# Layer 3 of a fused four-layer kernel: values in tiles of 128 tokens, taken through DRAM

## The chip, the cores and the metric

One core of a Trainium2 chip. The metric is the device time of one execution in microseconds, as the median of several runs; beside it stands one execution taken with the hardware profiler. All data are float32.

## The reference

Four residual layers over x of shape (4, 56, 56, 256): x = x + layer(group norm of x). Layers 0 and 2 are neighbourhood attentions, layer 1 is an all-to-all similarity over tokens, layer 3 is a shifted window attention. Layer 3, the one that the change is about, cut to what matters:

```python
xs = jnp.roll(x, (-3, -3), axis=(1, 2))                    # x: normalised, (4, 56, 56, 256)
xw = windows_of_7x7(xs)                                    # (4 * 64, 49, 256)
qkv = xw @ qkv_weight.T + qkv_bias
q, k, v = split_in_8_heads_of_32(qkv);  q = q * 32 ** -0.5
attn = softmax(q @ k.T + bias + mask)                      # 49 x 49 in each window and head
out = (attn @ v) @ proj_weight.T + proj_bias
x = x + roll_back(out)
```

## The kernel before, in words

The four layers run one after the other on one core; x goes through DRAM between them, with the 256 channels as two halves (`CC` = 2) of 128 partitions and the tokens along the free axis. A Python helper, `run` at the end of the program, opens each layer's pools and traces it. The framework sets semaphores, lays out memory and orders instructions by a cost model; layers 1 and 3 take the order of the engines named in their `run` call from the text instead. For layer 3 these are TensorE (PE), VectorE (DVE), ScalarE (ACT) and GpSimd (POOL). The queue that issues the DMAs, SP, is ordered by the cost model in all layers.

Layer 3 handles an image (3136 tokens) in 8 rows of 8 windows, `WC` = 392 tokens a row, 32 rows in all. In a row the windows lie in pairs of 98 tokens.

- `load(r)` brings the tokens of a row from DRAM, `prepare(r)` normalises them into `xn` in the order of the windows (line 939, DVE), six operations for the two halves.
- `project_rows(r)` gives six steps: keys, queries and values, each twice. Keys and queries are 128 x 392 outputs (`project`, line 945), taken out of PSUM by ACT (lines 1983, 1987). Values, `value_rows` (lines 956 to 965), are computed with the tokens as output partitions: for each pair of windows one accumulation of 98 tokens by 256 channels (line 962), two pairs per step, taken out by one DVE addition of the bias (line 964) into a tile `v` of 98 partitions by 4 pairs by 256. Each matmul of float32 is two records in the trace.
- `quad(r, hq)` is one unit of attention: four heads of a row, four window pairs. `attend_quads` runs the units, two per row and 64 in all: the logits of unit w (line 1025), the closing step `done` of the unit before the last (reciprocal, line 2006, and multiplication, line 2008, on DVE), then the unit's list of filling steps, then the products of unit w - 1 with the values and with ones (line 1040). Exponentials are on ACT (1029, 1031), the mask is added on DVE (1030) for two heads and multiplied on POOL (1032) for the other two.
- `stream` writes the filling steps of each unit: a step of the output projection of row r - 2 (`project_out`, PE line 945, ACT 2028, POOL 2030), three of the six steps of row r + 1, and in the second unit of a row `prepare(r + 2)`.

So in each unit PE runs: logits, output projection, keys, queries, values, products. PSUM banks for all projections come from one pool `m` of two banks; the products have one double bank `o`. Tiles of the pool `early` outlive the seam between layers (`x`, `xn`, `w_qkv` of layer 3), which lets them be filled while layer 2 still runs; which addresses a layer's pools get depends on their sizes, since the pools of odd layers are packed from the other end of the memory than those of even layers, and a tile waits for the old tiles that it lies on.

Layers 0 and 2 compute values in another helper, `value_tiles` (lines 973 to 993): tiles of 128 tokens counted from the start of the image, without regard to the rows. Where a row ends inside a tile, the rest (`left`) is copied by ACT in front of the next row's `xn`. A step a = 0 or 1 does up to two tiles. After step 1 the row's tiles go to a DRAM tile `vd` in one DMA (line 991), and a second (993) for the half tile at the end of an image; the attention gathers its keys' values from there (lines 1237 and 1790).

The lines that a sentence can't say, from `stream`:

```python
rows = lazily(project_rows, r + 1, 6) if r + 1 < n else []
out = project_out(r - 2) if r > 1 else []
for hq in range(CC):
    steps = out[hq:hq + 1] + rows[3 * hq:3 * hq + 3]
    if hq and r + 2 < n:
        steps.append(lambda r=r: prepare(r + 2))
    steps.append(step_stats)
```

Of the kernel before, what the change touches and what calls it, by code (L numbers as in the profile page):

```python
# [830 lines left out]
def direct_blocks(ctx: ExitStack, tc: tile.TileContext, d: dict, watch):  # L831
# [121 lines left out]
        else:  # L953
            nc.scalar.copy(dst, src)

    def value_rows(v, a, n, xn, w, bias):

        pm = ps_m()
        for j in range(2):
            k = 2 * a + j  # L960
            for h in range(CC):
                nc.tensor.matmul(pm[:n, j * C:(j + 1) * C], lhsT=xn[:, h, k * n:(k + 1) * n],  # L962
                                 rhs=w[:, h, :], start=(h == 0), stop=(h == CC - 1))
        nc.vector.tensor_tensor(v[:, 2 * a:2 * a + 2, :], pm[:n, :].rearrange("p (j c) -> p j c", c=C),
                                bias[:n].rearrange("p (o c) -> p o c", o=1).to_broadcast([n, 2, C]), ALU.add)

    def left(c, n):

        return c * n % P

    def value_tiles(v, a, c, n, xn, w, bias, dst):

        t0, t1 = c * n // P, (c + 1) * n // P if (c + 1) * n < T else -(-T // P)
        pm = ps_m()
        sizes = [min(P, T - t * P) for t in range(t0, t1)]
        mine = sizes[2 * a:2 * a + 2]
        for j, k in enumerate(mine):
            first = (2 * a + j) * P  # L980
            for h in range(CC):
                nc.tensor.matmul(pm[:k, j * C:(j + 1) * C], lhsT=xn[:, h, first:first + k], rhs=w[:, h, :],  # L982
                                 start=(h == 0), stop=(h == CC - 1))
        for k in sorted(set(mine)):
            js = [j for j, kj in enumerate(mine) if kj == k]
            nc.vector.tensor_tensor(
                v[:k, 2 * a + js[0]:2 * a + js[-1] + 1, :], pm[:k, js[0] * C:(js[-1] + 1) * C].rearrange("p (j c) -> p j c", c=C),
                bias[:k].rearrange("p (o c) -> p o c", o=1).to_broadcast([k, len(js), C]), ALU.add)
        if a == 1:
            whole = sizes.count(P)  # L990
            nc.sync.dma_start(out=dst[t0 * P:(t0 + whole) * P, :].rearrange("(k p) c -> p k c", p=P), in_=v[:, :whole, :])
            if whole < len(sizes):
                nc.sync.dma_start(out=dst[(t0 + whole) * P:T, :], in_=v[:sizes[-1], whole, :])

    def seen(rs):

# [937 lines left out]
    def layer3(early, big, pool, brief):  # L1934
        def image_rows(wr):

            return [(0, 7, 7 * wr + 3)] if wr < 7 else [(0, 4, S - 4), (4, 3, 0)]

        def transfer(l, r, x, out):
            b, wr = divmod(r, 8)  # L1940
            for i0, n, r0 in image_rows(wr):
                ends = x[:, :, i0 * S:(i0 + n) * S], tokens_of(l, b, r0 * S, n * S)
                nc.sync.dma_start(out=ends[out], in_=ends[1 - out])

        xs, xns, qkv, attns = {}, {}, {}, {}

        def load(r):
            xs[r] = early.tile([P, CC, WC], FP, tag="x", name="x3")
            transfer(3, r, xs[r], 0)

        load(0)
        w_qkv = weight(early, "wqkv3", 3 * C)
        m3 = big.tile([98, 2, NH, 4 * 98], FP, name="m3l")
        nc.sync.dma_start(out=m3, in_=m3d.rearrange("p a h w k -> p a h (w k)"))
        w_p = weight(pool, "wp3", C)

        def parts(win, x):

            win = win.rearrange("p (w i j) -> p w i j", i=7, j=7)
            img = x.rearrange("p (r c) -> p r c", c=S)  # L1960
            yield (win[:, 0:7].rearrange("p w i j -> p i w j"), img[:, :, 3:52].rearrange("p r (w j) -> p r w j", j=7))
            yield win[:, 7, :, 0:4], img[:, :, 52:56]
            yield win[:, 7, :, 4:7], img[:, :, 0:3]

        def prepare(r):
            x = xs.pop(r)
            if r + 1 < NIMG * 8:
                load(r + 1)
            xn = xns[r] = early.tile([P, CC, WC], FP, tag="xn", name="xn3")
            for h in range(CC):  # L1970
                for w, xv in parts(xn[:, h, :], x[:, h, :]):
                    normalise(w, xv, known(3, r // 8), h)

        def project_rows(r):
            xn = xns.pop(r)
            qT = pool.tile([P, CC, WC], FP, tag="q", name="q3")
            kT = pool.tile([P, CC, WC], FP, tag="k", name="k3")
            v = pool.tile([98, 4, C], FP, tag="v", name="v3")
            qkv[r] = qT, kT, v

            def keys(m):
                pm = project(w_qkv, C + m * P, lambda h: xn[:, h, :], WC)
                nc.scalar.activation(kT[:, m, :], pm, AF.Identity, bias=bk3[:, m:m + 1])

            def queries(m):
                pm = project(w_qkv, m * P, lambda h: xn[:, h, :], WC)
                nc.scalar.activation(qT[:, m, :], pm, AF.Identity, bias=qbias[:, 2, m:m + 1], scale=SCALE)

            def values(a):
                value_rows(v, a, 98, xn, w_qkv[:, :, 2 * C:], bv3)  # L1990

            return [lambda f=f, m=m: f(m) for m in range(2) for f in (keys, queries, values)]

        def quad(r, hq):
            b, wr = divmod(r, 8)
            qT, kT, v = qkv[r]
            box = {}

            def output(k, u):
                if k + u == 0:  # L2000
                    box["o"] = psum_tile("o", 1, 2)
                return box["o"][:, k, u * 98:(u + 1) * 98]

            def finish():
                rs = pool.tile([P, WC], FP, tag="rs", name="rs3")
                nc.vector.reciprocal(rs, box["o"][:, 1, :WC])
                seen(rs)
                nc.vector.scalar_tensor_tensor(attns[r][:, hq, :], box["o"][:, 0, :WC], 1.0, rs, ALU.mult, ALU.mult,
                                               accum_out=watch[2][:, 2 * r + hq:2 * r + hq + 1])

            def piece(u):
                sl = slice(u * 98, (u + 1) * 98)
                return (lambda j: kT[hr(j), hq, sl], lambda j: qT[hr(j), hq, sl],
                        lambda j: v[:, u, (4 * hq + j) * HD:(4 * hq + j + 1) * HD], True, True)

            mk = m3[:, wr // 7, 4 * hq:4 * hq + 4, :]
            i = 2 * (NIMG * 8 + r) + hq
            return dict(pieces=[piece(u) for u in range(4)], nk=98, nq=98, width=WC, mask=mk[:, 0:2, :],
                        emask=mk[:, 2:4, :], sum=watch[2][:98, i:i + 1], o=output, first=no_step, done=finish)

        def project_out(r):
            x = pool.tile([P, CC, WC], FP, tag="xr", name="xr3")
            transfer(3, r, x, 0)

            def step(m):
                pm = project(w_p, m * P, lambda h: attns[r][:, h, :], WC)
                pr = pool.tile([P, WC], FP, tag="pr", name="pr3")
                nc.scalar.activation(pr, pm, AF.Identity, bias=bp3[:, m:m + 1])  # L2028
                for w, xv in parts(pr, x[:, m, :]):
                    nc.gpsimd.tensor_tensor(xv, xv, w, ALU.add)  # L2030
                if m:
                    transfer(4, r, x, 1)
            return [lambda m=m: step(m) for m in range(CC)]

        def stream():
            n = NIMG * 8
            for r in range(n):
                attns[r] = pool.tile([P, CC, WC], FP, tag="attn", name="attn3", bufs=3)
                rows = lazily(project_rows, r + 1, 6) if r + 1 < n else []
                out = project_out(r - 2) if r > 1 else []  # L2040
                for hq in range(CC):
                    steps = out[hq:hq + 1] + rows[3 * hq:3 * hq + 3]
                    if hq and r + 2 < n:
                        steps.append(lambda r=r: prepare(r + 2))
                    steps.append(step_stats)
                    w = quad(r, hq)
                    w["fill"] = lambda steps=steps: [f() for f in steps]
                    yield w

        prepare(0)  # L2050
        prepare(1)
        for step in project_rows(0):
            step()
        attend_quads(pool, stream())
        for r in range(NIMG * 8 - 2, NIMG * 8):
            for step in project_out(r):
                step()
# [125 lines left out]
```

## Time and profile before

| | us |
|---|---|
| three runs | 4051.37, 4060.95, 4060.51 |
| their median | 4060.51 |
| the profiled execution, its own time | 4046.79 |
| its span in the trace | 4044.6 |
| layer 2: first matmul of its values | 2806.5 |
| layer 3: first matmul of its keys | 3492.4 |
| layer 3: last start of an output projection | 4035.8 |
| PE busy, of the span | 3858.0 (95%) |
| DVE, ACT, POOL busy | 2364.8, 1375.9, 1741.2 |
| granted PE clock, mean | 0.978 |

All times in the trace count from the span's start. PE, PEld are TensorE's matmuls and its loads of weights, which overlap; a matmul's length is modelled and overlaps its neighbours, so that the distance of starts says more than the mean. "Idle before" is time that an engine stood still ahead of an operation, with what ended it. Names of tiles stand as out<-in, with numbers left out; shapes are partitions x elements. A stage row has PE, PEld, DVE, ACT and POOL busy in a stretch (with the number of instructions), then the granted PE clock, the DMA engines' busy share and GB/s.

### The profile page before, as it was taken

How to read it: one execution, taken by the hardware profiler on the slowest of the kernel's cores; microseconds unless marked ns; L12 is line 12 of the kernel's file. 1: busy time of each engine (PE TensorE's matmuls, PEld its weight loads, DVE VectorE, ACT ScalarE, POOL GpSimd, SP SyncE). 2: the span in 40 equal slices, each digit the busy share in tenths (PEclk: the TensorE clock that was granted, in tenths of full speed). 3: DMA queues.
4: the chain of work that ended last, by engine and by line, in shares of the span. 5: the costliest groups of instructions: out<-in, count | busy, mean ns of one | idle time of the engine just before them, and what ended most of it. 6: DMA issues, size and time to landing. Idle time of an engine off the chain costs nothing.

```text
span 4044.6 us, 92225 instructions
## 1 busy us (share of the span) xinstructions
PE 3858.0 (95%) x38983; PEld 2715.6 (67%) x38983; DVE 2364.8 (58%) x4427; ACT 1375.9 (34%) x2899; POOL 1741.2 (43%) x1883
## 2 busy tenths in 40 slices
PE   6999999899999999999999999999999999999998
PEld 4566666557777577775777757776676676666665
DVE  6777777634444444444344543445788877666665
ACT  3355555322222122222222212222555555344443
POOL 2566767621123211232112321123676777545544
PEclk9899999899999999999999999999999999999999
DMA  8443333320000000000000000001444443322221
GB/s 266 102 133 121 114 118 105 104 85 6 24 23 29 25 6 24 15 29 25 6 24 15 29 19 10 10 10 50 126 128 131 125 119 113 102 73 73 74 77 62
DMA packets 241072, 276.12 MB, mean 68 GB/s; under 512 B 23430, under 2 KB 233000, under 8 KB 240168
## 3 DMA queue, kind: packets, MB, share of 16 engines
q1 hardware_dynamic: 240362, 270.06, 21.5%
q8 instruction: 308, 5.05, 0.5%
q14 instruction: 114, 0.93, 0.1%
q10 hardware_dynamic: 288, 0.08, 0.0%
HBM read 190.55 MB, written 79.53 MB: 67 GB/s over the span
## 4 chain that ended last, share of the span: by engine, by line
PE 48%; DVE 4%; POOL 2%; issue 1%; SPq 0%; DMA 0%; ACT 0%; DVEq 0%; POOLq 0%; ACTq 0%
PE ps_m L945 12%; PE ps_o L1505 6%; PE ps_s L1421 6%; PE ps_v L1510 6%; PE ps_o L1100 3%; PE ps_m L962 3%; PE ps_s L1071 3%; PE ps_o L1040 2%; PE ps_m L982 2%; PE ps_t L1491 1%; PE ps_s L1025 1%; DVE rs L1796 1%; PE ps_m L1389 1%; DVE xn L939 0%; DVE e L1078 0%
## 5 line engine op out<-in xcount | busy, mean ns | idle before, releaser
L1433 DVE TENSOR_TENSOR acc<-acc,ps_v 128x257 f32<-128x257 f32 x1104 | 455.8, 421 | 686.5 <-PE ps_v L1510 671.7
L1510 PE MATMUL ps_v<-xw,e 128*128 128x257 f32 x2208 | 613.1, 382 | 19.7 <-DVE acc L1433 18.0
L1505 PE MATMUL ps_o<-xw,at 128*128 128x257 f32 x2208 | 609.0, 379 | 0.0
L1421 PE MATMUL ps_s<-xnT,xd 128*128 128x512 f32 (+3 forms) x1344 | 571.1, 547 | 0.0
L1494 ACT COPY at<-ps_t 128x512 f32<-128x512 f32 (+3 forms) x332 | 170.5, 514 | 1049.8 <-PE ps_t L1491 1049.8
L1510 PEld LDWEIGHTS ps_v<-xw,e 128*128 128x128 f32 x2208 | 408.6, 189 | 171.1 <-issue 80.4
L1091 POOL TENSOR_TENSOR b<-e 126x336 f32<-126x336 f32 (+5 forms) x512 | 500.0, 997 | 10.0 <-ACT e L1079 1.9
L1505 PEld LDWEIGHTS ps_o<-xw,at 128*128 128x128 f32 x2208 | 419.1, 190 | 60.1
L1414 POOL TENSOR_SCALAR xd<-xnT,vec 128x128 f32<-128x128 f32 x192 | 115.1, 610 | 632.2 <-PE ps_s L1421 629.7
L945 PE MATMUL ps_m<-xn,w_wqkv 128*128 128x392 f32 x1024 | 381.6, 507 | 3.9 <-DVE xr L1831 2.5
L1082 POOL TENSOR_TENSOR e<-e,m0t 126x672 f32<-126x672 f32 (+3 forms) x128 | 238.7, 1865 | 265.0 <-ACT e L1081 252.1
L1082 POOL TENSOR_TENSOR e<-e,bias 119x784 f32<-119x784 f32 (+5 forms) x128 | 244.4, 1909 | 180.9 <-ACT e L1081 179.7
L1421 PEld LDWEIGHTS ps_s<-xnT,xd 128*128 128x128 f32 x1344 | 225.5, 191 | 134.8 <-issue 126.2
L1424 ACT ACTIVATE e<-ps_s 128x512 f32<-128x512 f32 x336 | 185.3, 551 | 336.7 <-PE ps_s L1421 336.7
L1003 ACT ACTIVATE no<-rs 128x168 f32<-128x168 f32 (+2 forms) x256 | 93.9, 367 | 590.2 <-DVE rs L1796 273.2
L945 PEld LDWEIGHTS ps_m<-xn,w_wqkv 128*128 128x128 f32 x1024 | 190.0, 192 | 127.5 <-ACT pr L2028 17.2
L1100 PEld LDWEIGHTS ps_o<-e,vp 124*32 124x32 f32 (+3 forms) x8192 | 176.3, 110 | 141.6 <-issue 93.0
L1100 PE MATMUL ps_o<-e,vp 124*32 124x112 f32 (+3 forms) x8192 | 238.8, 253 | 6.2 <-POOL e L1082 4.4
L939 DVE TENSOR_SCALAR xn<-x,gst 128x28 f32<-128x28 f32 (+5 forms) x368 | 208.1, 619 | 35.2 <-PE ps_m L945 28.7
L1079 ACT ACTIVATE e<-e 126x672 f32<-126x672 f32 (+5 forms) x256 | 219.5, 857 | 19.0 <-DVE e L1078 6.0
L1796 DVE RECIPROCAL rs<-ps_o 128x196 f32<-128x196 f32 (+2 forms) x128 | 176.0, 1375 | 77.7 <-PE ps_o L1100 77.1
L1032 POOL TENSOR_TENSOR e<-e,m3l 98x784 f32<-98x784 f32 x64 | 118.2, 1846 | 235.7 <-ACT e L1029 212.5
(197 smaller groups left out, 6340.9 us busy)
## 6 DMA issues: line engine op xcount, KB each, us to landing
x<-xr SPq DMA_DIRECT2D x64, 392.0 KB
x<-in_x SPq DMA_DIRECT2D x53, 448.0 KB
x<-x SPq DMA_DIRECT2D x60, 392.0 KB
xr<-x SPq DMA_DIRECT2D x60, 392.0 KB
vd<-v SPq DMA_DIRECT2D x48, 384.0 KB
xr<-in_x SPq DMA_DIRECT2D x32, 392.0 KB
xr<-x SPq DMA_DIRECT2D x28, 448.0 KB
x<-xr SPq DMA_DIRECT2D x28, 448.0 KB
```

The source lines that it names most:

```text
L939: nc.vector.tensor_scalar(dst, src, gst[:, h, 0:1], gst[:, h, 1:2], ALU.subtract, ALU.mult)
L945: nc.tensor.matmul(pm[:, :n], lhsT=w[:, h, col:col + P], rhs=rhs(h), start=(h == 0), stop=(h == CC - 1))
L1079: nc.scalar.activation(ev, ev, AF.Exp)
L1082: nc.gpsimd.tensor_tensor(parts(ev), parts(ev), w["emask"], ALU.mult)
L1091: nc.gpsimd.tensor_tensor(w["b"][a][:nk, :, :2 * nq].rearrange("p h (i c) -> p h i c", i=2), ev[:, :, :, 0, :], ev[:, :, :, 1, :], ALU.add)
L1100: nc.tensor.matmul(w["o"](k, i)[j * HD:(j + 1) * HD], lhsT=ones[:nk, :HD] if k else v(j, u), rhs=w["b"][j // 2][:nk, j % 2, i * nq:(i + 1) ...
L1421: nc.tensor.matmul(s[:, :n], lhsT=xd[j][:, h, :], rhs=xnT[:, h, first * P:last * P], start=(h == 0), stop=(h == CC - 1))
L1424: nc.scalar.activation(e[:, :n], s[:, :n], AF.Exp, scale=5.0)
L1433: nc.vector.tensor_tensor(acc[:, i, :], acc[:, i, :], pv[:, :C + 1], ALU.add)
L1505: nc.tensor.matmul(out[j][:, :C + 1], lhsT=e[:, col(i)] if i == j else at[:, col(i)], rhs=xw[:, i, :], start=(i == j), stop=(i == NB - 1))
L1510: nc.tensor.matmul(pv[:, :C + 1], lhsT=e[:, col(i)], rhs=xw[:, j, :], start=True, stop=True)
L1796: nc.vector.reciprocal(rs.rearrange("p (t c) -> p t c", t=2), pv[:, :, 1, :])
```

## The change

`value_rows` goes; layer 3 computes its values with `value_tiles`, as layers 0 and 2 do, and takes them through DRAM.

- `xn` becomes 448 wide with three buffers; `prepare` normalises behind the rest of the row before and copies that rest in front (ACT). It runs one row earlier, three ahead of the attention.
- `values(r)` makes the row's three tiles (four at the end of an image) in two steps, two rows ahead of the attention, into a tile `vt` of one buffer, and writes them to `vd`. With step 0 of a row the row before is complete, and `gather` reads its 392 tokens back as 98 partitions by 4 pairs, the form that the products take, into `vs`.
- `project_rows` keeps keys and queries (four steps). In a unit the steps stand as: output projection, keys, queries, values, `prepare`.
- Ahead of the first unit stand the values of rows 0 and 1, then keys and queries of row 0, then `prepare(2)`.
- `value_tiles` itself writes to DRAM after each addition and no longer once per row. Layers 0 and 2 use it too: in the built program their stores to `vd` are 128 where they were 68.

```diff
 def value_tiles(v, a, c, n, xn, w, bias, dst):
...
             bias[:k].rearrange("p (o c) -> p o c", o=1).to_broadcast([k, len(js), C]), ALU.add)
-        if a == 1:
-            whole = sizes.count(P)
-            nc.sync.dma_start(out=dst[t0 * P:(t0 + whole) * P, :].rearrange("(k p) c -> p k c", p=P), in_=v[:, :whole, :])
-            if whole < len(sizes):
-                nc.sync.dma_start(out=dst[(t0 + whole) * P:T, :], in_=v[:sizes[-1], whole, :])
+            t = t0 + 2 * a + js[0]
+            nc.sync.dma_start(out=dst[t * P:min((t + len(js)) * P, T), :].rearrange("(k p) c -> p k c", p=k),
+                              in_=v[:k, 2 * a + js[0]:2 * a + js[-1] + 1, :])
...
-        xs, xns, qkv, attns = {}, {}, {}, {}
+        xs, xns, vs, qk, attns, ahead = {}, {}, {}, {}, {}, []
+        vd = [dram.tile([T, C], FP, name=f"vd3_{b}") for b in range(NIMG)]
...
-            xn = xns[r] = early.tile([P, CC, WC], FP, tag="xn", name="xn3")
+            c = r % 8
+            xn = xns[r] = early.tile([P, CC, 448], FP, tag="xn", name="xn3", bufs=3)
+            at = left(c, WC)
             for h in range(CC):
-                for w, xv in parts(xn[:, h, :], x[:, h, :]):
+                for w, xv in parts(xn[:, h, at:at + WC], x[:, h, :]):
                     normalise(w, xv, known(3, r // 8), h)
+            if at:
+                end = left(c - 1, WC) + WC
+                nc.scalar.copy(xn[:, :, :at], ahead[0][:, :, end - at:end])
+            ahead[:] = [xn]
...
-            def values(a):
-                value_rows(v, a, 98, xn, w_qkv[:, :, 2 * C:], bv3)
-
-            return [lambda f=f, m=m: f(m) for m in range(2) for f in (keys, queries, values)]
+            return [lambda f=f, m=m: f(m) for m in range(2) for f in (keys, queries)]
+
+        def gather(r):
+
+            b, c = divmod(r, 8)
+            vs[r] = pool.tile([98, 4, C], FP, tag="v", name="v3")
+            nc.sync.dma_start(out=vs[r], in_=vd[b][c * WC:(c + 1) * WC, :].rearrange("(k p) c -> p k c", p=98))
+
+        def values(r):
+
+            b, c = divmod(r, 8)
+            xn = xns[r]
+            v = pool.tile([P, 4, C], FP, tag="vt", name="vt3", bufs=1)
+
+            def step(a):
+                value_tiles(v, a, c, WC, xn, w_qkv[:, :, 2 * C:], bv3, vd[b])
+                if a == 0 and r:
+                    gather(r - 1)
+                if a and r == NIMG * 8 - 1:
+                    gather(r)
+            return [lambda a=a: step(a) for a in range(2)]
...
-                rows = lazily(project_rows, r + 1, 6) if r + 1 < n else []
+                rows = lazily(project_rows, r + 1, 4) if r + 1 < n else []
+                ahead_values = lazily(values, r + 2, 2) if r + 2 < n else []
                 out = project_out(r - 2) if r > 1 else []
                 for hq in range(CC):
-                    steps = out[hq:hq + 1] + rows[3 * hq:3 * hq + 3]
-                    if hq and r + 2 < n:
-                        steps.append(lambda r=r: prepare(r + 2))
+                    steps = out[hq:hq + 1] + rows[2 * hq:2 * hq + 2] + ahead_values[hq:hq + 1]
+                    if hq and r + 3 < n:
+                        steps.append(lambda r=r: prepare(r + 3))
                     steps.append(step_stats)
...
         prepare(0)
         prepare(1)
+        for r in range(2):
+            for step in values(r):
+                step()
         for step in project_rows(0):
             step()
+        prepare(2)
         attend_quads(pool, stream())
```

More of the change, by code (lines that the diff above doesn't have):

```diff
@@ L954, in evac @@
             nc.scalar.copy(dst, src)
[L956 to L965, printed above, removed]
     def left(c, n):
@@ L1968, in prepare @@
                 load(r + 1)
-            xn = xns[r] = early.tile([P, CC, WC], FP, tag="xn", name="xn3")
+            c = r % 8
+            xn = xns[r] = early.tile([P, CC, 448], FP, tag="xn", name="xn3", bufs=3)
+            at = left(c, WC)
             for h in range(CC):
-                for w, xv in parts(xn[:, h, :], x[:, h, :]):
+                for w, xv in parts(xn[:, h, at:at + WC], x[:, h, :]):
                     normalise(w, xv, known(3, r // 8), h)
+            if at:
+                end = left(c - 1, WC) + WC
+                nc.scalar.copy(xn[:, :, :at], ahead[0][:, :, end - at:end])
+            ahead[:] = [xn]
         def project_rows(r):
-            xn = xns.pop(r)
+            at = left(r % 8, WC)
+            xn = xns.pop(r)[:, :, at:at + WC]
             qT = pool.tile([P, CC, WC], FP, tag="q", name="q3")
             kT = pool.tile([P, CC, WC], FP, tag="k", name="k3")
-            v = pool.tile([98, 4, C], FP, tag="v", name="v3")
-            qkv[r] = qT, kT, v
+            qk[r] = qT, kT
             def keys(m):
@@ L1987, in queries @@
                 nc.scalar.activation(qT[:, m, :], pm, AF.Identity, bias=qbias[:, 2, m:m + 1], scale=SCALE)
-            def values(a):
-                value_rows(v, a, 98, xn, w_qkv[:, :, 2 * C:], bv3)
-            return [lambda f=f, m=m: f(m) for m in range(2) for f in (keys, queries, values)]
+            return [lambda f=f, m=m: f(m) for m in range(2) for f in (keys, queries)]
[14 more added lines that the diff above has]
+            return [lambda a=a: step(a) for a in range(2)]
         def quad(r, hq):
             b, wr = divmod(r, 8)
-            qT, kT, v = qkv[r]
+            qT, kT = qk[r]
             box = {}
@@ L2013, in piece @@
                 return (lambda j: kT[hr(j), hq, sl], lambda j: qT[hr(j), hq, sl],
-                        lambda j: v[:, u, (4 * hq + j) * HD:(4 * hq + j + 1) * HD], True, True)
+                        lambda j: vs[r][:, u, (4 * hq + j) * HD:(4 * hq + j + 1) * HD], True, True)
             mk = m3[:, wr // 7, 4 * hq:4 * hq + 4, :]
```

## The prediction

> **What bounds the kernel now.** I first read the busy table by stage, to see which engine has no idle time where the change acts; then the groups of layer 3 by shape; then the waits of TensorE there; then single units in the timeline; last the seam between layers 2 and 3. Columns of a stage row: PE, weight loads, DVE, ACT, POOL busy, granted clock, DMA share, GB/s.
>
> ```profile
> 3570.00:3640.00 70.00, 70.00 (x1026) 48.08 (x1018) 46.84 (x67) 29.07 (x52) 33.55 (x41) 1.00 0.22 71
> ```
>
> In 70 us of layer 3 TensorE is busy for 70.00 at full clock; DVE has 23 us free, DMA runs at 0.22. The waits of PE from 3500 us to the end agree: one releaser of note, three times, at the tail.
>
> ```profile
> PE ps_o L1040 <- DVE attn L2008: 8.2, 3, 3.5
> ```
>
> So a matmul less is time less, unless the freed time meets another limit. The groups of layer 3 (busy us, mean ns, idle before):
>
> ```profile
> L962 PE MATMUL ps_m<-w_wqkv,xn 128*98 128x256 f32 x480 | 113.6, 379 | 0.0
> L964 DVE TENSOR_TENSOR v<-ps_m,bc 98x512 f32<-98x512 f32 x60 | 41.5, 692 | 127.0 <-PE ps_o L1040 75.4 <-PE ps_m L962 51.6
> ```
>
> The mean of 379 ns overlaps its neighbours; the price is the spacing. One unit of the timeline (half a row of windows):
>
> ```profile
> 3703.13 0.95 PE L1025 MATMUL ps_s<-q,k 32*98 32x98 f32 x32
> 3704.01 1.58 PE L945 MATMUL ps_m<-attn,w_wp 128*128 128x392 f32 x4
> 3705.43 2.80 PE L945 MATMUL ps_m<-xn,w_wqkv 128*128 128x392 f32 x8
> 3707.70 0.57 DVE L2008 SCALAR_TENSOR_TENSOR attn<-ps_o,rs 128x392 f32<-128x392 f32 x1
> 3708.06 1.89 PE L962 MATMUL ps_m<-w_wqkv,xn 128*98 128x256 f32 x8
> 3709.88 0.89 PE L1040 MATMUL ps_o<-e,v 98*32 98x98 f32 x32
> 3711.38 0.95 PE L1025 MATMUL ps_s<-q,k 32*98 32x98 f32 x32
> ```
>
> A unit takes 3711.38 - 3703.13 = 8.25 us, 64 of them make the layer. Eight value records take 1.89 us, 0.236 us each. The division of DVE (`attn`) is over at 3708.27, 1.61 us before the products need its bank.
>
> Whether a record with 128 tokens costs more than one with 98 is seen in layer 2, which has that shape:
>
> ```profile
> 3165.71 1.99 PE L982 MATMUL ps_m<-w_wqkv,xn 128*128 128x256 f32 x8
> 3167.54 1.48 PE L945 MATMUL ps_m<-xn,w_wqkv 128*128 128x392 f32 x4
> ```
>
> The next group starts 1.83 us later: eight of them cost no more.
>
> The floor of a unit is seen in row 31, where no projection fills the gap:
>
> ```profile
> 4008.26 0.95 PE L1025 MATMUL ps_s<-q,k 32*98 32x98 f32 x32
> 4013.55 0.89 PE L1040 MATMUL ps_o<-e,v 98*32 98x98 f32 x32 [2.83 <-DVE attn L2008]
> 4015.05 1.64 PE L1025 MATMUL ps_s<-q,k 32*98 32x98 f32 x32
> ```
>
> It is 6.79 us, set by DVE (mask addition, reciprocal 2.60 us, division).
>
> **The Trainium skill.** "TensorE: Matmul & The Clock Gate", section "LDWEIGHTS (loading the stationary operand)", says a weight load takes time by its columns, not its rows of contraction. The trace agrees in direction: 190 ns with 128 columns, 165 ns with 98; both are below 236 ns of spacing. Its section "HAM oscillation — how this bites in real kernels" says idle gaps of some 3.4 us bring the clock down to half. The seam between the layers has such gaps, and a granted clock of 0.71 behind them:
>
> ```profile
> 3494.00:3498.00 4.00, 4.00 (x12) 2.38 (x11) 0.00 (x0) 1.17 (x2) 0.00 (x0) 0.71 0.76 217
> ```
>
> "DMA: Bandwidth & Descriptors", section "Two DMAs through the same engine are not ordered", says a reader of what a DMA wrote must wait for that DMA's semaphore, the same queue isn't enough: the new gather thus pays one whole landing of its store. The trace before has the same order through DRAM in layer 2, so its landing times serve here.
>
> **The change, part by part.**
> *Value matmuls.* Before, an image has 32 window pairs, two halves of the contraction each, two records each: 128 records, 512 in four images. After: 3136 tokens are 25 tiles, 100 records, 400 in all (the built order of TensorE shows 4, 2, 4, 2 matmuls per unit for 4, 4, 4, 4). 112 x 0.236 = 26.5 us less. Ahead of the first logits stand now rows 0 and 1, 24 records, for 16; so the stream of units loses 120 records = 28.4 us, and the 1.9 us more at the start are booked there.
> *Does each unit shrink?* The first unit of a row keeps two tiles, 8.25 us. The second has one tile: 8.25 - 0.95 = 7.30 us, above the floor of 6.79, and `attn` is ready 0.66 us before the products. Full credit. (Row 7 of an image has four tiles and keeps both units long; the records above count that.) Row 30 has no values left: 8.25 - 1.89 = 6.36, under the floor, loss 2 x 0.43 = 0.9 us.
> *DVE.* 692 ns per unit become 0.69 and 0.41 us (layer 2 has the 256-wide form at 0.41). Off the path; if that cover went, it would still be a gain.
> *ACT.* 28 copies of up to 56 tokens; layer 2 shows 0.23 us for 64. ACT idles 3.63 us before each exponential, which hides it; uncovered 28 x 0.23 = 6.4 us.
> *SP and DMA, layer 3.* 68 stores and 32 gathers at about 0.4 us are 40 us on a queue that has some 530. The gather waits for its store, and for the products that free `vs`; behind it stand the output store, the second store and the loads of `x` and `xr`. A landing is 2.6 us (mean wait of `xr` for `out_x`, 79.2 us in 31). The gather of row r+1 is asked for in the first unit of row r and read in the second of row r+1: three units, over 20 us. `xr` is loaded one row ahead. `vt` has one buffer, so the next evacuation waits for both stores of the row before; they land some 3 us into the unit, the evacuation comes at 6.9. Behind it on DVE stand the next row's normalisation and the mask addition, for which the products of the unit after wait. All hidden, 0; bounds: below nothing is excluded, as no wait is removed from PE here; above, 0.3 us x 32 rows = 10.
> *Layers 0 and 2.* They use the same helper: 128 stores for 68, each behind its own evacuation. PE barely waits for gathers now (14 us in 26 waits). Its order there is the same but for a few swaps at the start of layer 0. Taken at 0, from -3 (values land earlier) to +6 (60 x 0.4 us of issue, a quarter of it felt).
> *The seam.* Here I see the cost. Before, layer 3 was prepared long ahead:
>
> ```profile
> L1943 SPq DMA_DIRECT2D x<-x x36: 359/422/1486, 2923.3 to 3962.7; - x36
> L881 SPq DMA_DIRECT2D w_wqkv<-in_wqkv x2: 456/457/458, 802.6 to 2836.8; - x2
> ```
>
> `xn` takes three buffers of 3584 bytes for two of 3136. This moves the layer's tiles down by 4480 bytes, `x3` now lies over layer 2's `v2`, and in the built order the load of `x` row 0, of w_wqkv and both normalisations stand behind layer 2's last gather. At that place the trace has:
>
> ```profile
> 3474.09 0.42 SPq L1954 DMA_DIRECT2D m3l<-m3d x1
> 3478.00:3482.00 4.00, 2.26 (x72) 1.39 (x66) 2.86 (x5) 1.60 (x4) 3.61 (x4) 1.00 1.01 357
> 3488.15 0.42 SPq L1828 DMA_DIRECT2D xr<-x  x1
> 3491.74 1.16 DVE L1831 SCALAR_TENSOR_TENSOR xr<-ps_m,vec,xr 128x392 f32<-128x392 f32 x2 [3.12 <-issue]
> 3492.41 4.59 PE L945 MATMUL ps_m<-xn,w_wqkv 128*128 128x392 f32 x8 [2.45 <-DVE xr L1831]
> ```
>
> Layer 3 started at 3492.4 and its first logits at 3503.0. Now: x(0) and w_wqkv (1.18 MB) leave at 3474.1 and are there by 3479. m3l (2.4 MB) goes behind a store at 3479.3 and holds the engines to about 3489. `x` row 1 leaves behind `xr`, 3488.6, and lands near 3493 (`xr` took 3.6). DVE: layer 2's last additions to 3494.3, xn(1) 1.67 us to 3496.0, evacuations of row 0 to 3497.1. Their stores land at 3500; only then `vt` is free for row 1, to 3501.1. Keys and queries of row 0 need those banks: four groups of 1.4 us, logits at 3506.8. The gaps lower the clock (these first eight records took 4.59 us for 2.80), and m3l may delay `x` more: I take 3510, 7 us late. Bounds: 1.9 (the added records alone), 15 (all loads in series and a second landing).
>
> **Sum**, against the profiled execution of 4046.79 us (span 4044.6): -28.4 + 0.9 + 7 = -20.5, so 4026.3. The median of the runs, 4060.51, lies 13.7 above that execution; the same step from it gives 4040.0. The three runs spread by 10 us.
>
> **Rivals.**
> *The seam costs double* (m3l and x in series, clock down): 18 us late; 28.4 - 0.9 - 18 = 9.5 gain, 4051. For it: 357 GB/s there already. Against: DVE still has layer 2's rest to do until 3492.
> *The units don't shrink*: a round trip of DRAM shows each row (`vt` or the gather late by 0.6 us, 32 times 19 us less the rest): gain about 2 to 8, 4055. Against: the slacks above, 3 us and more.
> *Slower: the split stores clog SP in layers 0 and 2.* A store that waits for its evacuation holds up the gathers behind it; SP waits there 56 us in 27 such cases now, 2 us each. 60 more would be 120 us of SP; if a third reaches PE, +40: 4060.5 - 20.5 + 40 = 4080. It decides once PE feels more than 20.5 us, 0.34 us for each added store. Against: the scheduler puts them between gathers that have a unit of lead.
> *The change doesn't do what it says*: the built order shows the 400 records; this one is out.
>
> **Numbers.** The likeliest, 4040 (4030 to 4048), 0.72; seam doubled 0.12; no shrinking 0.09; slower 0.07. A step of 0.3% (12.2 us) is about what runs of this kernel can tell from none. Faster 0.75, same 0.17, slower 0.08: the doubled seam and the unshrunk units end within 0.3%, but for 0.03 and 0.01 at their edges. The range takes in the doubled seam and, below, a seam of 1.9 us with values early: 4028 to 4054.
>
> **What would show it.** Right: 400 value records; pairs of units 8.25 + 7.30 = 15.55 us in seven rows of eight; PE without waits from 3520 to the tail; first logits 5 to 10 us later, loads of `x` and w_wqkv near 3474. Wrong: PE waiting for `v` or `vt` in each row; POOL waiting for `xr`; waits for gathers in layers 0 and 2 grown from 14 us to over 30; a seam beyond 3518.

## The result, and the profile after

The changed kernel takes 4033.3 us (median of 12 runs, 4024.02 to 4045.55); the kernel before, run beside it 12 times, 4050.04 us. The ratio is 0.9956, 95% interval 0.9944 to 0.9967: 18 us less, between 13 and 23. The profiled execution took 4042.54 us, its span 4040.7 at a mean granted clock of 0.974. It is one of the longest of the twelve: their spans go from 4022.2 us at a clock of 0.978 to 4043.8 at 0.973. This spread is as large as the step, and already at the first values of layer 2 this execution stands 10.6 us later than the profile of before (2817.12 for 2806.50), ahead of any layer 3. So stretches are compared below, not ends.

The stage of 70 us inside layer 3 (columns as in the prediction), then the waits of TensorE from 3500 us on (us in total, times, longest):

```profile
3570.00:3640.00 70.00, 69.98 (x1026) 48.39 (x1025) 46.78 (x68) 30.20 (x56) 36.13 (x45) 1.00 0.41 123
```

```profile
PE ps_o L1027 <- DVE attn L2019: 9.5, 4, 3.5
PE ps_m L945 <- DVE vt L975: 4.2, 1, 4.2
PE ps_m L971 <- DVE xr L1818: 3.7, 1, 3.7
```

TensorE is still busy throughout. The DMA share went from 0.22 to 0.41 and no wait for `v` came with it: the first line is the tail, as before, the two others happen once each, in the seam. The groups of values from 3500 us on:

```profile
L971 PE MATMUL ps_m<-w_wqkv,xn 128*128 128x256 f32 x384 | 95.0, 385 | 3.7 <-DVE xr L1818 3.7
L975 DVE TENSOR_TENSOR vt<-ps_m,bc 128x512 f32<-128x512 f32 x32 | 22.1, 692 | 58.3 <-PE ps_m L971 52.5 <-DMA vd<-vt 5.8
```

With the 16 records of 64 tokens that is 400, and DVE waited for a store of `vt` in one place only. One row of the stream, its two units from logits to logits:

```profile
3690.76 0.95 PE L1012 MATMUL ps_s<-q,k 32*98 32x98 f32 x32
...
3695.70 1.89 PE L971 MATMUL ps_m<-w_wqkv,xn 128*128 128x256 f32 x8
3697.52 0.89 PE L1027 MATMUL ps_o<-e,v 98*32 98x98 f32 x32
...
3699.01 0.95 PE L1012 MATMUL ps_s<-q,k 32*98 32x98 f32 x32
...
3703.95 1.03 PE L971 MATMUL ps_m<-w_wqkv,xn 128*128 128x256 f32 x4
3704.90 0.89 PE L1027 MATMUL ps_o<-e,v 98*32 98x98 f32 x32
...
3706.40 0.95 PE L1012 MATMUL ps_s<-q,k 32*98 32x98 f32 x32
```

The first unit keeps its 8.25 us, the second is 7.39. The last rows stand on the floor of DVE: 6.79 and 6.74 us in row 30, and 6.80 in row 31:

```profile
4004.62 0.95 PE L1012 MATMUL ps_s<-q,k 32*98 32x98 f32 x32
...
4011.42 0.95 PE L1012 MATMUL ps_s<-q,k 32*98 32x98 f32 x32
```

From the first logits to these last ones the stream took 488.1 us for 512.0. The other side is the seam between layers 2 and 3. The queue of SP there, then TensorE and the one late evacuation:

```profile
3483.08 0.47 SPq L1930 DMA_DIRECT2D x<-x  x1
3483.60 0.46 SPq L881 DMA_DIRECT2D w_wqkv<-in_wqkv  x1
```

```profile
3491.91 7.91 PE L945 MATMUL ps_m<-attn,w_wp 128*128 128x392 f32 x16
3503.55 7.37 PE L971 MATMUL ps_m<-w_wqkv,xn 128*128 128x256 f32 x24 [3.73 <-DVE xr L1818]
3515.10 8.26 PE L945 MATMUL ps_m<-xn,w_wqkv 128*128 128x392 f32 x16 [4.17 <-DVE vt L975]
3523.29 0.95 PE L1012 MATMUL ps_s<-q,k 32*98 32x98 f32 x32
```

```profile
3514.36 1.02 DVE L975 TENSOR_TENSOR vt<-ps_m,bc 128x512 f32<-128x512 f32 x2 [5.81 <-DMA vd<-vt]
```

The loads that before went out at 2923 and 2837 us stand behind layer 2's last gather, as the built order said. I measure the seam from the start of layer 2's last 16 projection records to the first logits: 31.4 us here, 20.6 before, between these two lines:

```profile
3482.41 7.56 PE L945 MATMUL ps_m<-attn,w_wp 128*128 128x392 f32 x16
...
3503.02 0.95 PE L1025 MATMUL ps_s<-q,k 32*98 32x98 f32 x32
```

The seam of after holds two waits of TensorE, for the last residual sum (`xr`) and for row 1's `vt`. The clock is low in parts of it, among them layer 2's last projections, ahead of the first wait, and the keys and queries behind the second:

```profile
3494.00:3498.00 4.00, 4.00 (x9) 2.03 (x8) 2.27 (x7) 0.24 (x2) 0.00 (x0) 0.66 0.91 289
3514.00:3518.00 4.00, 2.90 (x5) 1.64 (x6) 2.60 (x8) 0.00 (x0) 0.00 (x0) 0.50 0.31 105
```

So -23.9 us in the stream and +10.8 in the seam: -13.1 in this pair of profiles.

### The profile page after: what moved, and what is told of

Read it like the earlier page. It is cut to its first block, busy times and chain, and to the rows that moved or that the text cites. A ratio compares the mean times of both kernels' runs of the same rounds, so it can differ in the third digit from the quotient of the medians.

```text
span 4040.7 us, 92344 instructions
## 1 busy us (share of the span) xinstructions
PE 3848.9 (95%) x38871; PEld 2716.9 (67%) x38871; DVE 2356.6 (58%) x4431; ACT 1381.2 (34%) x2927; POOL 1746.3 (43%) x1883
## 4 chain that ended last, share of the span: by engine, by line
PE 48%; DVE 4%; POOL 2%; issue 1%; DMA 0%; ACT 0%; POOLq 0%; DVEq 0%; SPq 0%; ACTq 0%
PE ps_m L945 13%; PE ps_o L1492 6%; PE ps_s L1408 6%; PE ps_v L1497 6%; PE ps_m L971 4%; PE ps_o L1087 3%; PE ps_s L1058 3%; PE ps_o L1027 2%; PE ps_t L1478 1%; PE ps_s L1012 1%; DVE rs L1783 1%; PE ps_m L1376 1%; PE ps_m L1363 0%; DVE e L1065 0%; DVE rs L2017 0%
## 5 line engine op out<-in xcount | busy, mean ns | idle before, releaser
L939 DVE TENSOR_SCALAR xn<-x,gst 128x28 f32<-128x28 f32 (+4 forms) x368 | 204.5, 609 | 33.1 <-PE ps_m L945 29.0
```

What stands on the lines that cost most here:

```text
L939: nc.vector.tensor_scalar(dst, src, gst[:, h, 0:1], gst[:, h, 1:2], ALU.subtract, ALU.mult)
```

## The experiments

The theory: the stream is bound by TensorE and pays for missing records alone, the seam takes part of it back, and neither the way through DRAM nor the split stores cost anything. Its rivals: the later place or earlier preparation of the step pays by itself; DRAM or the stores cost something. All kernels were read at the same marks, one profiled execution each ("waits": TensorE for `xr`, then for `vt`):

| kernel | seam us | waits in it us | stream us | ratio to before |
|---|---|---|---|---|
| before | 20.6 | 2.45, none | 512.0 | 1 |
| after | 31.4 | 3.73, 4.17 | 488.1 | 0.9956 |
| after, again | 27.5 | 3.91, 2.62 | 488.6 | 0.9955 |
| before, split stores | 20.7 | 2.55, none | 512.0 | 0.9993 |
| before, wide xn | 22.4 | 4.10, none | 512.8 | 1.0017 |
| order only | 25.7 | 3.87, none | 510.0 | 0.9992 |
| values twice | 29.2 | 4.03, none | 569.3 | 1.0151 |
| gather a row later | 31.3 | 3.84, 4.17 | 488.8 | 0.9949 |
| one v | 31.3 | 4.17, 3.82 | 488.1 | 0.9954 |
| one x3 | 25.5 | 2.94, 2.07 | 487.6 | 0.9936 |
| two vt3 | 24.7 | 5.31, none | 488.8 | 0.993 |
| both | 23.1 | 3.05, none | 487.8 | 0.9934 |
| both, again | 23.1 | 2.95, none | 489.1 | 0.994 |

**Split stores alone.** The kernel before with the new stores in layers 0 and 2:

```diff
-        if a == 1:
-            whole = sizes.count(P)
...
+            t = t0 + 2 * a + js[0]
+            nc.sync.dma_start(out=dst[t * P:min((t + len(js)) * P, T), :].rearrange("(k p) c -> p k c", p=k),
+                              in_=v[:k, 2 * a + js[0]:2 * a + js[-1] + 1, :])
```

> The kernel before with the stores of values in layers 0 and 2 written after each addition (128 for 68), layer 3 as before. My forecast was no effect: ratio 1.000, within 0.1%. Rival one (the split lets gathers start sooner): 3 to 5 us less, ratio 0.999. Rival two (the stores clog the DMA queue): ratio over 1.002, waits of PE for gathers above 30 us (14 before).

Measured 0.9993 (0.9981 to 1.0004), 4047.97 us: no difference that the times can tell, 8 us less or 2 more at the ends of the interval. The slower rival of the prediction wanted 40 us more; it is out. A gain of 3 to 5 us, rival one, lies inside the interval and isn't ruled out by the times. In layer 2 the trace shows none: from its first values to the mark of the seam there are 675.9 us in both kernels.

**Wide `xn` alone.** The kernel before, only its `xn3` as large as in after, with the values as they were:

```diff
-            xn = xns[r] = early.tile([P, CC, WC], FP, tag="xn", name="xn3")
+            xn = xns[r] = early.tile([P, CC, 448], FP, tag="xn", name="xn3", bufs=3)[:, :, :WC]
```

> The kernel before with xn in three buffers of 448 tokens, of which only 392 are used: nothing of the values is changed, only the memory of the layer's early tiles. My theory: the loads move behind layer 2's last gather, first logits 35 to 40 us after it (29.0 before), time 6 to 11 us over the kernel before, ratio 1.0015 to 1.0027. Rival (late loads cost nothing by themselves): ratio 1.000.

Measured 1.0017 (1.0006 to 1.0028), 4055.46 us. Not one instruction of the computation is added, and yet the first load of layer 3 has gone behind layer 2's last gather:

```profile
3475.78 0.46 SPq L1943 DMA_DIRECT2D x<-x  x1
```

So memory's layout alone moves the loads, and costs some 7 us by the times (2 to 11). Where most of that is lost isn't shown: this profile has 1.8 us more in the seam and 0.8 in the stream, and its first logits stand 31.4 us behind layer 2's last gather, where 35 to 40 were expected.

**Order only.** After without tiles of 128 and without DRAM, but two rows ahead and last in a unit:

```diff
-            v = pool.tile([P, 4, C], FP, tag="vt", name="vt3", bufs=1)
+            v = vs[r] = pool.tile([98, 4, C], FP, tag="v", name="v3", bufs=4)
 
             def step(a):
-                value_tiles(v, a, c, WC, xn, w_qkv[:, :, 2 * C:], bv3, vd[b])
...
+                value_rows(v, a, 98, xn, w_qkv[:, :, 2 * C:], bv3)
```

> After without its tiles of 128 and without DRAM: the values of layer 3 are made again in 16 records a row from 98 tokens each and stay on the chip (four buffers), but two rows ahead and last in a unit as in after, with the wide xn in three buffers. Theory (only the 120 missing records pay, the place of the step is worth nothing): a unit of 8.25 us in both halves of a row as before; in the stream 480 records for 496, 16 x 0.215 = 3.4 us less, 0.9 us more for row 30 at the floor of DVE; ahead of the first logits 32 records for 16, which with the late loads makes the seam 4 to 9 us longer than before. Sum +1.5 to +6.5 us, ratio 1.0004 to 1.0016. Rival (that the values stand last and early itself gives half of the gain in the stream or more, 12 us): units under 8.1 us, ratio 0.9985 or less.

Measured 0.9992 (0.9978 to 1.0006), 4046.75 us. The interval reaches the low end of the theory and the upper end of the rival, so the time decides nothing. The trace does; the logits of three units:

```profile
3700.92 0.95 PE L1023 MATMUL ps_s<-q,k 32*98 32x98 f32 x32
...
3709.17 0.95 PE L1023 MATMUL ps_s<-q,k 32*98 32x98 f32 x32
...
3717.41 0.95 PE L1023 MATMUL ps_s<-q,k 32*98 32x98 f32 x32
```

Both units are 8.25 us, as before. The place of the step is worth nothing in the stream.

**Values twice.** After with each value matmul of layer 3 made twice:

```diff
-            for h in range(CC):
+            for h in [*range(CC)] * times:
...
-                value_tiles(v, a, c, WC, xn, w_qkv[:, :, 2 * C:], bv3, vd[b])
+                value_tiles(v, a, c, WC, xn, w_qkv[:, :, 2 * C:], bv3, vd[b], 2)
```

> After with every value matmul of layer 3 made twice in a row, the second time over the first: 800 records for 400, 376 of the added ones in the stream; nothing else is added. Theory (a record is worth 0.215 us of spacing, as the two kinds of units say): units of 9.97 and 8.25 us for 8.25 and 7.39, the stream 81 us longer, the seam some 3 to 6; ratio 1.0162 to 1.0172. Rival (0.236 us a record, the value on record, which was a group's duration divided by eight): units of 10.14 and 8.33, the stream 89 us longer, ratio 1.018 to 1.019.

Measured 1.0151 (1.0127 to 1.0174), 4107.47 us: the theory lies in the interval, the rival's 1.018 doesn't. The units:

```profile
3701.88 0.95 PE L1012 MATMUL ps_s<-q,k 32*98 32x98 f32 x32
...
3706.81 3.62 PE L971 MATMUL ps_m<-w_wqkv,xn 128*128 128x256 f32 x16
...
3711.85 0.95 PE L1012 MATMUL ps_s<-q,k 32*98 32x98 f32 x32
...
3720.10 0.95 PE L1012 MATMUL ps_s<-q,k 32*98 32x98 f32 x32
```

9.97 and 8.25 us: eight records more are 1.72 us, four are 0.86, that is 0.215 each. The stream grew by 569.3 - 488.6 = 80.7 us, 376 x 0.215 = 80.8. In the seam the doubled records fill the time in which TensorE had waited for `vt`: it grew by 1.7 us only against the repeated run beside it.

**The way through DRAM.** First each gather a whole row later:

```diff
-                if a == 0 and r:
-                    gather(r - 1)
-                if a and r == NIMG * 8 - 1:
-                    gather(r)
...
+                    if hq == 0:
+                        steps.append(lambda r=r: gather(r))
```

> After with each gather a whole row later: the gather of row r stands in the first unit of row r itself, behind the store of row r+2, and is read by the products at the end of the next unit. Theory (in after the row lies ready some 17 us ahead of its products, so 15.6 us later it still is): units 8.25 and 7.39 us as in after, TensorE waits for v in no row, ratio 0.9956 (0.9948 to 0.9966). Rival (the way through DRAM is hidden by the two rows of lead alone): 1 to 3 us in each of 32 rows, ratio 1.003 to 1.02.

Measured 0.9949 (0.9933 to 0.9966), 4033.39 us, as after. The gather and the products that read it:

```profile
3707.97 0.33 SPq L1989 DMA_DIRECT2D v<-vd  x1
...
3712.35 0.89 PE L1027 MATMUL ps_o<-e,v 98*32 98x98 f32 x32
```

4.4 us lie between them and TensorE doesn't wait for `v`; in after the same distance is 3720.84 - 3700.95 = 19.9 us. Then with a single buffer for `v3`, and the gather in the second unit:

```diff
-            vs[r] = pool.tile([98, 4, C], FP, tag="v", name="v3")
+            vs[r] = pool.tile([98, 4, C], FP, tag="v", name="v3", bufs=1)
...
+                    if hq:
+                        steps.append(lambda r=r: gather(r))
```

> After with one buffer for v3 and the gather asked for in the second unit of its row: it can leave only when the products of the row before are done, one unit (7.4 us) ahead of its own, and it holds up the queue of SP until then. Theory (a landing of 2.6 to 3.5 us, with 5.9 us to the products): still hidden, units as in after, ratio 0.9956 (0.9945 to 0.997); SP waits for PE some 5 us in each row, and the loads behind it come later but have a row of lead. Rival (the landing or the held queue reaches TensorE): 2 us or more in each row, ratio 1.011 or more.

Measured 0.9954 (0.9932 to 0.9976), 4032.3 us. The gather leaves at 3706.00, when the row before is done, and is read at 3712.03; units as in after. The queue of SP was expected to wait for TensorE some 5 us in each row; it came to 19.2 us in 30 waits over the whole stream. So less than a unit between gather and products hides the way through DRAM, and the rival of units that don't shrink is out. A gather so late that it shows was not tried.

**The seam, one part each.** One buffer for `x3` (the tiles of layer 3 move back up and the loads go out early), two for `vt3` (row 1 need not wait for row 0's stores), both:

```diff
-            xs[r] = early.tile([P, CC, WC], FP, tag="x", name="x3")
+            xs[r] = early.tile([P, CC, WC], FP, tag="x", name="x3", bufs=1)
```

> The changed kernel with one buffer for x of layer 3 in place of two; the layer's early tiles then end above layer 2's value tile again, and in the built order the loads of w_wqkv and of the first rows stand far ahead of layer 2's end, as before the change. My theory (the stream of units gains 24 us, the seam gives 11 of them back because the early loads lost their place): first logits of layer 3 some 30 us after layer 2's last gather (changed kernel 40.2, kernel before 29.0), time 26 to 29 us under the kernel before, ratio 0.9930 to 0.9937. Rival (the seam costs what the extra values ahead of the first unit cost, not the place of the loads): no change from the changed kernel, ratio 0.9956.

```diff
-            v = pool.tile([P, 4, C], FP, tag="vt", name="vt3", bufs=1)
+            v = pool.tile([P, 4, C], FP, tag="vt", name="vt3", bufs=2)
```

> The changed kernel with two buffers for vt. The evacuation of row 1's values at the seam then doesn't wait for the stores of row 0 (DVE waited 5.8 us, PE 4.2 us for it). My theory: 4 us less than the changed kernel, ratio 0.9946, units of the stream as they are. Rival (that wait only covers others: landing of x, the low clock): under 1 us, ratio 0.9956.

> After with one buffer for x3 and two for vt3 together. Theory (the two edits take away two waits of one chain): the run with one x3 still waited 2.07 us for vt, this goes; what is left of the seam against before is 8 records more (1.7 us) and some clock, 2 to 4 us in all. Ratio 0.9931 (0.9927 to 0.9936), 2 us under the run with x3 alone. Rival (the gains add: 10.8 us of loss less 5.9 less 6.8): ratio 0.992. Rival 2 (a second vt makes room for nothing else): as with x3 alone, 0.9936.

> The changed kernel as it is, beside the next one on one chip: 0.9956 (0.9944 to 0.9967) again. It shows whether the two edits of the seam are worth anything that the times can tell.

> The changed kernel with one buffer for x3 and two for vt3, once more. Theory (the seam alone differs: 2.5 us longer than before for 10.8 in after, the stream the same): 8 us under the changed kernel beside it, ratio 0.9934 to 0.9938 for its 0.9956. Rival (the loss of the seam is only moved, to the spread of the granted clock): no difference between the two.

Measured: one `x3` 0.9936 (0.9922 to 0.995), as the theory had it, though the first logits stand 34.4 us behind the last gather (40.2 in after), where 30 were expected; two `vt3` 0.993 (0.9915 to 0.9944), more than expected (0.9946); both 0.9934 (0.9917 to 0.9952) and 0.994 (0.9923 to 0.9958). TensorE's values and its keys and queries of row 0 with one `x3`, then its keys and queries with both:

```profile
3496.80 7.13 PE L971 MATMUL ps_m<-w_wqkv,xn 128*128 128x256 f32 x24 [2.94 <-DVE xr L1818]
3506.01 5.53 PE L945 MATMUL ps_m<-xn,w_wqkv 128*128 128x392 f32 x16 [2.07 <-DVE vt L975]
```

```profile
3499.73 5.53 PE L945 MATMUL ps_m<-xn,w_wqkv 128*128 128x392 f32 x16
```

With one `x3` the loads are out of the way, and the two stores of row 0 land 3.1 us after they are issued for 5.4 in after (DVE goes on at 3505.26 after issues that end at 3502.18, and at 3514.36 after 3508.99). The wait halves, and the keys and queries behind it take 5.53 us for 8.26. With two `vt3` the wait is gone altogether. But the second profile of after, with its loads in the same late place, has 3.7 us for the stores, a wait of 2.62 and 5.53 us for the keys and queries as well. So how much of this is due to the place of the loads, and how much differs from one execution to the next, isn't shown.

Against the first profile of after the two edits take 5.9 and 6.7 us off the seam, together 8.3, and don't add; against the second it is 2.0, 2.8 and 4.4, and they nearly do. A longer stretch says the same: from layer 2's first values to layer 3's first logits before took 696.5 us, the two profiles of after 706.2 and 700.3, one `x3` 703.4, two `vt3` 701.6, both 699.1 and 699.3. Only both together stand under either profile of after. That the second `vt` gained more than was expected may be the clock, since I had counted the wait alone, or the spread of the runs.

Do the times show it? After alone and both edits differ by 0.0015 to 0.0022 in ratio; in neither of the two pairs do the intervals part, and in the pair that ran side by side the medians are 1.7 us apart (4030.34 and 4028.66). The means of the two ratios each, 0.9956 and 0.9937, differ by 0.0018, with about 0.0015 of uncertainty (the half-widths combined). It is likely, not shown, that the version with both is faster than after, by some 7 us; faster than before it is in both its runs.

## Why the prediction was right, point by point

**The stream: mechanism right, term mis-sized.** The prediction put 120 records x 0.236 = 28.4 us, less 0.9 for row 30. It came to 23.9. The 0.236 was the duration of a group of eight, 1.89 us, divided by eight. But that duration holds the end of the last record, beside which the next group has already begun. The distance to the next group's start doesn't give the price either: it is 1.82 us for eight (3695.70 to 3697.52) and 0.95 for four (3703.95 to 3704.90), 0.23 and 0.24 each. About 0.1 us belongs to a group whatever its size, and stays when records go. What four records less save is the difference of the two kinds of units, 0.86 us, 0.215 each. 120 x 0.215 = 25.8.

The rest of the way to 23.9 is in single units. An image's last row has 64 tokens in a group of their own; its second unit is 8.39 us for 8.25, 0.14 x 4 = 0.6 us. With 0.5 for row 30 (below), 24.7 are left; two units of 8.55 and 8.68 where others have 8.25 and 8.39 make 0.6, and the first four units, 1.4 us shorter for 8 records fewer, 0.3. These parts sum to the 23.9 measured.

The price stood in the profile of before: in layer 2 a group of eight is 1.83 us from the next group, as the prediction shows, and a group of four 0.97, which is 0.86 us for four:

```profile
3170.98 1.13 PE L982 MATMUL ps_m<-w_wqkv,xn 128*128 128x256 f32 x4
3171.95 1.48 PE L945 MATMUL ps_m<-xn,w_wqkv 128*128 128x392 f32 x4
```

**The second unit.** 7.30 expected, 7.38 to 7.39 measured, by the same error. It shrank in every ordinary row, as the prediction said, and is 0.6 us above the floor of 6.79.

**The floor in row 30.** Two units of 6.79 and 6.74 us, where 8.25 - 1.72 = 6.53 would have been without it: 0.5 us for the two, 0.9 were put.

**The seam: right in place and cause, its terms mis-sized.** Put at 7 us, bounds 1.9 and 15; by the profiles 10.8 and, in the second profile of the same kernel, 6.9 (27.5 - 20.6). The two runs with a later gather, whose seam is built alike, have 31.3 us as well. Counted from the mark, the prediction had row 0's evacuations over after 14.7 us, their stores landed 2.9 later, and four groups of 1.4 us for the keys and queries, 5.7 up to the logits. The first profile has 16.6, 5.8 and 8.2 us, 7 us more in all (0.4 came back between them), and the 3.2 us kept back for the clock and for m3l cover less than half of it. The second has 17.3, 4.1 and 5.5, 3.1 us more in all, which the 3.2 just cover. TensorE had waited 4.17 us ahead of the keys and queries in the first, 2.62 in the second, and the clock was low behind the longer wait. The first logits at 3523.29 stand beyond 3518, a sign of being wrong that the prediction names; but this execution is 10.6 us late ahead of layer 2, and from its own mark the seam is 10.8 us longer, under the 15 that were meant.

**Zero terms.** Gathers, stores and copies in the stream, 0: shown by the run with the gather a row later and by the one with one `v`. Split stores in layers 0 and 2, 0: the run with them alone can't be told from before, and the waits of TensorE's weight loads for gathers are 8.5 us in 16 waits in the profile after (14 in 26 before), where the prediction named 30 as the sign of trouble. The copies on ACT (0.19 to 0.28 us each) show in no wait of TensorE.

**The sum.** -20.5 was predicted; the ratio gives -17.8, the profiles -13.1 and -16.5. Two misses, 3.6 us in the stream and up to 3.8 in the seam, made the gain too large. That the median, 4033.3, lies below the forecast of 4040.0 all the same is due to its base: the three runs of before that it was added to had a median of 4060.51, nine more brought it to 4050.04. Put on this base the same step gives 4029.5, which is 3.8 us under the median measured.

## What to carry to other kernels

Price a matmul that goes by the difference between groups of different size, or between whole periods with more and with fewer of them. A group's duration divided by its count was 10% too much here, and the distance to the next group divided by the count still 6 to 10%. A tile that grows can move its neighbours in memory, and here what they then overlapped decided when a stage's first loads could leave; read the built order of the loads at each stage boundary, not only the code that changed. Where the boundary has a single buffer between a store and the next evacuation, try a second one: here it was worth 6.7 us of the seam against one profile of after, where the wait was 4.17 us and the clock fell behind it, and 2.8 against the other, where it was 2.62. A stage boundary that takes 31.4 us in one execution and 27.5 in the next needs more than one profile before an edit there is judged.

## What the runs showed of the hardware

- After TensorE waited 4.17, 4.17 and 3.82 us for `vt`, the same 16 records (keys and queries of row 0) took 8.26, 8.21 and 8.32 us; after waits of 2.62 and 2.07 us, or with two `vt3` and no wait, 5.53. The length of the wait alone doesn't decide it: in before a wait of 2.45 us for `xr` was followed by eight records of keys and queries in 4.59 us for 2.80. The Trainium skill, "TensorE: Matmul & The Clock Gate", section "HAM oscillation — how this bites in real kernels", gives idle gaps of more than some 3.4 us as what lowers the clock; here the clock fell behind a shorter one. It is the wait ahead of the granted clock of 0.71 that the prediction shows. In the clock records of these traces the slow stretches of the seam last 3.41 or 6.83 us.
- A matmul record with 128 tokens and 256 columns costs 0.215 us in the stream whether it is taken away (0.86 us for four) or added (1.72 us for eight), and one with 98 tokens the same (units of 8.25 us with eight of either).
- A store of `vt` lands 2.3 us after its issue in the stream (the gather that waits for it left at 3700.95, the issue ended at 3698.70); the two behind the loads of `x`, w_wp and `xr` in the seam took 5.4 us in one profile of after and 3.7 in the other.
